# Two-layer graph attention on one core: a third buffer for the scaled features, the sums over A moved ahead at the end of the first pass, layer norm in two steps, and a row term in partial sums

## The chip, the cores and the metric

The kernel runs on one core of a Trainium2 chip. The metric is the device time of one execution in microseconds (us). The kernel before was timed three times: 2105.14, 2100.93 and 2103.20 us, median 2103.2 us.

## What is computed

Two layers over 4096 nodes with 512 features, each followed by a residual sum and a layer norm:

```python
feats = einsum('nf,hfo->hno', x, W)                 # 8 heads of 64
dense = s_self[:, :, None] + s_neigh[:, None, :]
dense = where(dense > 0, dense, 0.2 * dense) * A    # A: 4096 x 4096, zeros and ones
x = layernorm(x + relu(softmax(dense) @ feats + b)) # layer 0
q, k, v = x @ Wq.T + bq, x @ Wk.T + bk, x @ Wv.T + bv
a = where(mask, q @ k.T * scale, 0)                 # mask: same graph; 32 graphs of 128 nodes
scores = (a + A + A) * where(mask, 1, -1e6)
x = layernorm(x + (softmax(scores) * mask) @ v)     # layer 1
```

In layer 1 only the 32 diagonal blocks of 128 by 128 count. With M = Wq^T Wk the scores are x M x^T plus row terms; the one this change touches is `ub`, the product of bk with Wq, times the scale, needed as the same row of 512 numbers in all 128 partitions.

## The kernel before, in words

`adjacency_streamed_path` does the work; `general_path` is compiled but only entered for other kinds of input. Heads go in pairs: r = 0 to 3 is a pair, and a pass. In each pass the columns of A^T go in four chunks c of 1024, and in each chunk 32 tiles j of 128 rows.

**Setup** (lines 578 to 795). For each of eight blocks k of four tiles: load x, turn it (L635), multiply by W (L715, in `features`), add the bias into `fb` (L723). `scaled_features` (L726) makes two tiles from `fb`: `gst` (L729, VectorE) and `fst` (first half by ScalarE, L737, second half by VectorE, L738). Both are written to DRAM (`g_d`, `f_d`) by DMAs on GpSimd's queue (L750). `gst`, `fst`, `xT_f` and `pu_j` come from the pool `two` with two buffers; `fb` from `three` with three. The bits `exponentials` and `scores` for the attention need the copy `st` (L652) on ScalarE, and the small matmuls L658 read it. After blocks 3, 4 and 5 a load of four tiles of A, cast to fp8 (L573), goes into the same GpSimd queue.

**A pass** (`main_pass`, L1263). A step takes `wide` tiles j, eight in passes 0 to 2 and four in pass 3. In each step VectorE makes `q` (L1310) from `p_row`, `d_all` and the tile `at` of A^T; ScalarE (or VectorE, L1315) makes `mark` from `q`; TensorE accumulates `accf` (L1330) from `at` and `f_s`, then `acc` (L1347) from `q` and `g_s`, then `dens` (L1361) from the marks. In pass 0 it also accumulates `ae` (L1374) from `at`: the sums over A, written at the end of the step. `bring` gets the tiles `at` of the following step: in pass 0 by transposes (L1088) and copies (L1092), and for later passes by a load on SP's queue (L1078). In pass 0 half of these calls stand after `accf`, half at the end of the step, after `ae`. The twelve buffers of `at` (six in pass 3) go round; a buffer is free again when `accf`, `ae` and both `q` of its tile have been made.

**Ends of a chunk.** `sums_to_rows` first copies the accumulators (`ys` L1136 and L1144, `dcs` L1146, `aes` L1151), then hands back a generator of pieces, which are issued between the matmuls of the next chunk: `run_pieces` spends a credit of 0.75 us per tile and step, and each `yield` states a cost. During pass 1 the same credit pays for `weights_of_layer_1` (L864), whose last pieces are the column term `zb` (L908) and `ub` and `cb` (L918 to L929).

**Layer 1 in pass 3.** From the second chunk of pass 3 on, an order written out by hand is followed: `PLAN` names for each step what is issued after `accf` and what after `acc`. E ends a chunk and calls `rows_of_layer_0` (L1112: residual, relu, layer norm of four row tiles, made into `x1b`), R does so for its second half, a and b are the pieces of `layer_1` for these two. What is left after the last chunk is a string of the same letters (L1426). `rows_out` (L1039) writes rows, two tiles at a time, through `layernorm` (L518): statistics on VectorE (L524, L525), the power on GpSimd (L527, L528), the scaling on VectorE (L530).

**Order.** TensorE runs in the order of the source (L455). The other engines' orders, and those of the DMA queues, are fixed when the kernel is built, by a scheduler that works with modelled times and the order of the source.

```python
banks.append(banks.pop(0))          # misc(): PSUM banks in turn
queue = nc.sync if blk >= NT // 4 - 2 else nc.gpsimd   # rows_out: who writes the rows
for x_ in follow[first:]:           # end of a step: second half of the next tiles
    bring(*x_)
```

Of the kernel before, what the change touches and what calls it, by code (L numbers as in the profile page):

```python
# [10 lines left out]
F32 = mybir.dt.float32  # L11
BF16 = mybir.dt.bfloat16
# [7 lines left out]
P = 128  # L20
# [384 lines left out]
def adjacency_streamed_path(  # L405
# [112 lines left out]
    def layernorm(tiles):  # L518

        n = len(tiles)  # L520
        stats = small.tile([P, n, 6], F32, name="stats_f")
        mv = small.tile([P, n, 2], F32, name="mv_f")
        for u, src in enumerate(tiles):
            nc.vector.bn_stats(stats[:, u, :], src)  # L524
            nc.vector.bn_aggr(mv[:, u, :], stats[:, u, :])  # L525
        rstd = small.tile([P, n], F32, name="rstd_f")
        nc.gpsimd.tensor_scalar_add(rstd, mv[:, :, 1], EPS)  # L527
        nc.gpsimd.tensor_tensor(rstd, rstd, neg_half_4[:, :n], OP.pow)  # L528
        for u, src in enumerate(tiles):
            nc.vector.tensor_scalar(  # L530
                src, src, mv[:, u, 0:1], rstd[:, u : u + 1], op0=OP.subtract, op1=OP.mult
            )


    gfp = ctx.enter_context(tc.tile_pool(name="gs", bufs=2))
# [42 lines left out]
    with tc.tile_pool(name="setup1", bufs=1, side="right") as one, tc.tile_pool(  # L578
# [20 lines left out]
        for c in range(FC):  # L599
# [1 line left out]
                w_sb[:, c].rearrange("p (h o) -> p h o", h=H),  # L601
                W[:, ts(c, P), :].rearrange("h p o -> p h o"),
            )
        a_b2 = two.tile([P, PR, 2, FP], F32R, name="fst").bitcast(F32)
# [120 lines left out]

        def scaled_features(k, u, fb):  # L726
            j = 4 * k + u
            gst = two.tile([P, PR, 2, FH], F32, name="gst")
            nc.vector.tensor_tensor(  # L729
                gst.rearrange("p r h o -> p (r h) o"),  # L730
                fb,
                e_all[:, j, 1, :, None].to_broadcast([P, H, FH]),
                OP.mult,
            )
            fst = two.tile([P, PR, 2, FP], F32R, name="fst")
            fr = fb.rearrange("p (r h) o -> p r (h o)", h=2)
            nc.scalar.activation(fst[:, :, 0, :], fr, AF.Copy, scale=-1.0)  # L737
            nc.vector.scalar_tensor_tensor(  # L738
                fst[:, :, 1, :],
                fr,  # L740
                -1.0,
                fst[:, :, 0, :].bitcast(F32),
                op0=OP.mult,
                op1=OP.subtract,
            )
            for dst, n, src in (
                (g_d, FP, gst.rearrange("p r h o -> p r (h o)")),
                (f_d, 2 * FP, fst.rearrange("p r s n -> p r (s n)").bitcast(F32)),
            ):
                nc.gpsimd.dma_start(dst[:, k, :, ts(u, n)].rearrange("r p n -> p r n"), src)  # L750
# [113 lines left out]
    def weights_of_layer_1(keep, wp):  # L864

        L1["M"] = keep.tile([P, FC, F], F32, name="M_sb")
        L1["wvT"] = keep.tile([P, FC, F], F32, name="wvT")
        L1["zb"] = keep.tile([P, FC], F32, name="zb")
        L1["ub"] = keep.tile([P, F], F32, name="ub")
        L1["cb"] = keep.tile([P, 1], F32, name="cb")  # L870
        L1["bv"] = keep.tile([P, F], F32, name="bv_row")
        nc.sync.dma_start(L1["bv"], broadcast_rows(bv, P, F))
        cols = {}
        for name, v in (("q", bq), ("k", bk)):
            cols[name] = wp.tile([P, FC], F32, name="b_" + name)
            nc.sync.dma_start(
                cols[name],
                bass.AP(tensor=v.tensor, offset=v.offset, ap=[[1, P], [P, FC]]),
            )
        ws = {}  # L880
        for name, w in (("q", Wq), ("k", Wk), ("v", Wv)):
            yield 6.0
            ws[name] = wp.tile([P, FC, F], F32, name="w_" + name)
            nc.sync.dma_start(ws[name], w.rearrange("(c p) f -> p c f", p=P))
        yield 6.0
        for m in range(FC):
            pm = misc([P, F])
            for o in range(FC):
                nc.tensor.matmul(
                    pm,  # L890
                    ws["q"][:, o, ts(m, P)],
                    ws["k"][:, o, :],
                    start=(o == 0),
                    stop=(o == FC - 1),
                )
            nc.scalar.mul(L1["M"][:, m, :], pm, scale)
            yield 3.7
        for o in range(FC):
            pv = misc([P, FC, P])
            for k in range(FC):  # L900
                nc.tensor.transpose(pv[:, k, :], ws["v"][:, o, ts(k, P)], ident)
            nc.scalar.copy(L1["wvT"][:, :, ts(o, P)], pv)
            if o % 2:
                yield 1.3
        pz = misc([P, FC])
        for m in range(FC):
            for o in range(FC):
                nc.tensor.matmul(  # L908
                    pz[:, m : m + 1],
                    ws["k"][:, o, ts(m, P)],  # L910
                    cols["q"][:, o : o + 1],
                    start=(o == 0),
                    stop=(o == FC - 1),
                )
        nc.scalar.mul(L1["zb"], pz, scale)
        yield 2.0

        pu = misc([P, F])  # L918
        pc = misc([P, 1])
        kb = wp.tile([P, FC, P], F32, name="kb")  # L920
        nc.vector.tensor_copy(kb, cols["k"][:, :, None].to_broadcast([P, FC, P]))
        for dst, rhs in ((pu, ws["q"]), (pc, cols["q"][:, :, None])):
            for o in range(FC):
                nc.tensor.matmul(
                    dst, kb[:, o, :], rhs[:, o, :], start=(o == 0), stop=(o == FC - 1)
                )
        nc.scalar.mul(L1["ub"], pu, scale)
        nc.scalar.mul(L1["cb"], pc, scale)
        yield 4.5  # L929

    def layer_1(blk, x1b, lp, lp1, lp2):
# [107 lines left out]
        def rows_out(us):  # L1039
            ys = []  # L1040
            for u in us:
                po = misc([P, F])
                nc.tensor.matmul(po, pT[:, u, :], vs[u], start=True, stop=True)  # L1043
                y = lp.tile([P, F], F32, name="y_f")
                nc.vector.scalar_tensor_tensor(
                    y, po, rd[:, u : u + 1], x1b[:, u, :], op0=OP.mult, op1=OP.add
                )
                ys.append(y)
            layernorm(ys)
            for i, u in enumerate(us):  # L1050
# [14 lines left out]
        values(2)  # L1065
        values(3)
        yield
        rows_out((2, 3))
        yield


# [40 lines left out]
    def rows_of_layer_0(blk, hst, lp):  # L1112
        x1b = lp.tile([P, 4, F], F32, name="x1b")
        for u in range(4):
# [4 lines left out]
            for dst, src in (  # L1119
# [1 line left out]
                (x1b[:, u, F - FP :], hst[:, it % CT, :]),  # L1121
            ):
                nc.vector.scalar_tensor_tensor(dst, src, 0.0, dst, op0=OP.max, op1=OP.add)
        layernorm([x1b[:, u, :] for u in range(4)])
        return x1b

    def sums_to_rows(r, c, acc, accf, ae, u_row, later_by):
# [104 lines left out]

    PLAN = [("E", "b"), ("b", "b"), ("b", "a"), ("Ra", "a"), ("a", "b"), ("ba", "b")]
    PLANS = PLAN + [("ab", ""), ("aaba", "")], PLAN + [("a", ""), ("aa", "a")]
    plan = {"b": None}

    def run_plan(todo):
        for k in todo:  # L1240
            gen = ends[0] if k == "E" else plan[k]
            if gen is not None:
                next(gen)
            if k == "E":
                ends.pop(0)
# [17 lines left out]
    def main_pass(r, ae=None, wide=4):  # L1263

        for c in range(NCH):
# [10 lines left out]
            def pieces(c, group, place):  # L1276
                if r == PR - 1 and c:
                    run_plan(PLANS[c == NCH - 1][group][place])
                elif place == (r == 0):
                    run_pieces(0.75 * wide)  # L1280

            acc = psa.tile([P, 2, HB], F32, name="acc")
            accf = psa.tile([P, 2, HB], F32, name="accf")
            marks = {}
            for j0 in range(0, NT, wide):
# [41 lines left out]
                for j in cycle:  # L1327
                    for w in range(2):
                        for s in range(2):
# [4 lines left out]
                                start=(j == 0 and w == 0),  # L1334
                                stop=(j == NT - 1 and w == 1),
                            )
                first = wide // 2 if r == 0 or wide == 4 else 6
                for x_ in follow[:first]:
                    bring(*x_)
# [17 lines left out]
                for j in range(done_j - 8, done_j) if done_j % 8 == 0 else ():  # L1357
                    for s in range(2):
                        for h in range(2):
# [5 lines left out]
                                start=(j == 0),  # L1365
                                stop=(j == NT - 1),
                            )
                if r == 0:
                    for j in cycle:

                        a_j = ats[r, c, j].bitcast(BF16).rearrange("p (n k) -> p n k", k=2)
                        for s in range(2):
                            lo = 32 * (2 * (j % 2) + s)
                            nc.tensor.matmul(  # L1374
                                ae[lo : lo + NE + 1, :],
                                e_p[:, j, : NE + 1],
                                a_j[:, ts(s, HB), 1],
                                start=(j < 2),
                                stop=(j >= NT - 2),
                            )  # L1380
# [39 lines left out]
    with tc.tile_pool(name="lp", bufs=2) as lp, tc.tile_pool(  # L1420
# [2 lines left out]
        pools.update(lp=lp, lp1=lp1, lp2=lp2)  # L1423
        main_pass(3)
        plan["K"] = kind_of_inputs(lp1)
        run_plan("bbEbbbbaaRaaKKbbababaababbbb")  # L1426


@with_exitstack
# [50 lines left out]
```

## Time and profile before

| | |
|---|---|
| median of three executions | 2103.2 us (2100.93 to 2105.14) |
| the profiled execution, its own time | 2104.88 us |
| its span in the profile | 2102.9 us |
| TensorE (PE) busy | 2061.3 us, 98% of the span |
| VectorE (DVE) busy | 1659.0 us, 79% |
| ScalarE (ACT) busy | 1535.7 us, 73% |
| GpSimd (POOL) busy | 249.4 us, 12% |
| moved by DMA | 551 MB, mean 262 GB/s |
| setup | 0 to about 172 us |
| first `accf` of passes 0, 1, 3 | 177, 604, 1391 us |
| after the last chunk | 1981 to 2103 us |

In the profile a line names a source line, an engine, an operation, the tiles (out<-in), and then times. In the timeline the columns are start, busy time, engine, line, operation, tiles, count, and in brackets how long the engine had been idle before and what ended it. In a table of stretches there are, for each engine, busy us and (x) instructions, then PEclk, the share of full speed that TensorE's clock was granted, then the DMA's busy share and GB/s. SPq and POOLq are the queues in which SP and GpSimd issue DMAs. Float32 matmuls show as two instructions each.

### The profile page before, as it was taken

To read this page: it belongs to the slowest core of one execution; us is meant where nothing else is said; L and a number is where in the kernel's file an instruction comes from. 1 tells how busy PE (TensorE), PEld (TensorE's weight loads), DVE (VectorE), ACT (ScalarE), POOL (GpSimd) and SP (SyncE) were. 2 spreads that over 40 slices of the span, in tenths; PEclk is the share of its full clock that TensorE was granted. 3 is DMA by queue.
4 is the path that set the end of the run, shared out by engine and by line. 5 is a ranking of instruction groups with operands and counts; after the bars stand their busy time and mean duration, and the time that the engine had idled before them with its cause. 6 is when DMAs were issued, how large, how long until landed. Compare 5 with 4: busy or idle time off the path is not lost. (4 is left out here: it accounts for less than half of the span.)

```text
span 2102.9 us, 38131 instructions
## 1 busy us (share of the span) xinstructions
PE 2061.3 (98%) x15012; PEld 1015.0 (48%) x15012; DVE 1659.0 (79%) x2032; ACT 1535.7 (73%) x1818; POOL 249.4 (12%) x391
## 2 busy tenths in 40 slices
PE   8999999999999999999999999999999999999997
PEld 4545555454445544445444544444454444445443
DVE  5547788878788998787999989999975884886654
ACT  3327998888868889787899989998876666567420
POOL 2333222222100000000000000000300210210110
PEclk9999999999999999999999999999999999999999
DMA  8999999999889999887999999989964674675211
GB/s 246 270 211 243 287 285 271 294 263 278 263 286 327 338 361 344 297 301 239 323 324 343 311 327 337 334 281 362 305 238 152 239 243 144 225 270 163 73 48 42
DMA packets 207881, 551.28 MB, mean 262 GB/s; under 512 B 25292, under 2 KB 66252, under 8 KB 207692
## 3 DMA queue, kind: packets, MB, share of 16 engines
q1 hardware_dynamic: 140748, 425.79, 58.3%
q0 software_dynamic: 62784, 121.91, 23.3%
q8 instruction: 120, 1.97, 0.4%
q10 hardware_dynamic: 4160, 1.05, 0.2%
q14 instruction: 69, 0.57, 0.1%
HBM read 491.79 MB, written 107.22 MB: 285 GB/s over the span
## 5 line engine op out<-in xcount | busy, mean ns | idle before, releaser
L1310 DVE SCALAR_TENSOR_TENSOR q<-p_row,d_all,at 128x1024 f32<-128x1024 f32 x1024 | 1242.5, 1277 | 180.2 <-PE acc L1347 146.2
L1319 ACT ACTIVATE mark<-q,nb_all 128x1024 fp8e4<-128x1024 f32 x896 | 994.6, 1145 | 192.1 <-DVE q L1310 176.7
L1347 PE MATMUL acc<-q,g_s 128*32 128x512 f32 x8192 | 907.3, 594 | 3.3 <-DVE q L1310 2.9
L1347 PEld LDWEIGHTS acc<-q,g_s 128*32 128x32 f32 x8192 | 265.1, 110 | 599.2 <-issue 532.9
L1330 PE MATMUL accf<-at,f_s 128*128 128x512 f32 x2048 | 494.4, 397 | 5.5 <-DMA at<-at_d 3.9
L1330 PEld LDWEIGHTS accf<-at,f_s 128*128 128x128 f32 x2048 | 378.7, 188 | 116.0 <-issue 25.6
L1107 ACT ACTIVATE ck<-ck,neg_half_f 128x1024 f32<-128x1024 f32 x128 | 145.9, 1140 | 22.1 <-DMA ck<-in_adj_dram 22.1
L1108 ACT ACTIVATE ck<-ck,neg_quarter 128x1024 f32<-128x1024 f32 x128 | 146.3, 1143 | 1.8
L1092 ACT CAST at<-ps_m 128x1024 fp32r<-128x1024 fp8e4 x128 | 120.1, 1026 | 10.4 <-issue 5.9
L1361 PE MATMUL dens<-mark,e_b 128*6 128x512 fp8e4 x2048 | 125.0, 379 | 1.2 <-ACT mark L1319 1.2
L715 PE MATMUL ps_set<-w_sb_f,xT_f 128*128 128x512 f32 x256 | 116.4, 603 | 0.0
L957 PE MATMUL ps_m<-x1T,M_sb 128*128 128x512 f32 x256 | 113.1, 595 | 1.2 <-ACT x1T L938 1.2
L1029 PE MATMUL ps_m<-wvT,x1T 128*128 128x512 f32 x256 | 114.2, 594 | 0.0
L1212 POOL DMA_DIRECT2D hs_d<-hst x12 | 10.7, 895 | 849.6 <-DVE hst L1202 755.6
L1315 DVE TENSOR_SCALAR mark<-q,d_all 128x1024 fp8e4<-128x1024 f32 x128 | 95.7, 748 | 4.8
L737 ACT ACTIVATE fst<-fb 128x512 fp32r<-128x512 f32 x32 | 20.3, 633 | 101.5 <-DMA f_d<-fst 76.8
L1361 PEld LDWEIGHTS <-e_b 128*6 128x6 bf16 x2048 | 52.7, 86 | 81.0 <-issue 37.2
L1093 POOL DMA_DIRECT2D at_d<-at x128 | 68.7, 537 | 181.3 <-ACT at L1092 104.0
L957 PEld LDWEIGHTS ps_m<-x1T,M_sb 128*128 128x128 f32 x256 | 47.9, 190 | 62.7 <-issue 60.1
L1029 PEld LDWEIGHTS ps_m<-wvT,x1T 128*128 128x128 f32 x256 | 47.6, 190 | 57.2 <-issue 56.0
L715 PEld LDWEIGHTS ps_set<-w_sb_f,xT_f 128*128 128x128 f32 x256 | 49.1, 199 | 49.7 <-issue 49.4
L1037 DVE TENSOR_TENSOR v_t<-ps_m,bv_row 128x512 f32<-128x512 f32 x32 | 21.9, 684 | 62.2 <-PE ps_m L1029 62.2
(172 smaller groups left out, 1141.6 us busy)
## 6 DMA issues: line engine op xcount, KB each, us to landing
at<-at_d SPq DMA_DIRECT2D x384, 512.0 KB, 6.1
ck<-in_adj_dram SPq DMA_DIRECT2D x128, 512.0 KB, 5.4
f_s<-f_d SPq DMA_DIRECT2D x128, 512.0 KB, 7.6
at_d<-at POOLq DMA_DIRECT2D x128, 512.0 KB, 15.2
g_s<-g_d SPq DMA_DIRECT2D x128, 256.0 KB, 5.7
f_d<-fst POOLq DMA_DIRECT2D x32, 512.0 KB, 6.3
p_row<-pu_d SPq DMA_DIRECT2D x32, 512.0 KB, 7.1
a_b<-in_adj_dram POOLq DMA_DIRECT2D x32, 512.0 KB, 17.2
```

The source lines that it names most:

```text
L715: nc.tensor.matmul(pf, tile_j(xTs[k][:, c].rearrange("p u n -> p (u n)"), u), w_sb[:, c, :], start=(c == 0), stop=(c == FC - 1),)
L957: nc.tensor.matmul(pz, L1["M"][:, f, ts(c, P)], x1T[:, f, :], start=(f == 0), stop=(f == FC - 1),)
L1029: nc.tensor.matmul(pv, x1T[:, f, ts(u, P)], L1["wvT"][:, f, :], start=(f == 0), stop=(f == FC - 1),)
L1092: nc.scalar.copy(at, both[:, :, k])
L1107: tc.keep_in_program_order(nc.scalar.activation(ck, ck, AF.Square, bias=neg_half))
L1108: nc.scalar.activation(ck, ck, AF.Abs, bias=neg_quarter, accum_out=binp[:, k : k + 1])
L1310: nc.vector.scalar_tensor_tensor(q, p_row[h], d_j, ats[r, c, j].bitcast(F32), op0=OP.max, op1=OP.mult)
L1315: nc.vector.tensor_scalar(mark, q, d_j, None, op0=OP.is_gt, saturate=False)
L1319: nc.scalar.activation(mark, q, AF.Sigmoid, bias=nb_all[:, j, hh : hh + 1], scale=BIG, saturate=False,)
L1330: nc.tensor.matmul(accf[:, s, :], f_s[j // 4][:, j % 4, w, :], ats[r, c, j][:, ts(s, HB)], start=(j == 0 and w == 0), stop=(j == NT - 1 an ...
L1347: nc.tensor.matmul(acc[o : o + 32, s, :], g_s[j // 4][:, j % 4, h, o % FH : o % FH + 32], qs[j, h][:, ts(s, HB)], start=(j == 0), stop=(j ...
L1361: nc.tensor.matmul(dens[lo : lo + 6, :], e_b[:, j, 2 * r + h, :], marks[j, h][:, ts(s, HB)], start=(j == 0), stop=(j == NT - 1),)
```

## The change

Five edits:

1. `gst` and `fst`, and the tile at the start that shares `fst`'s buffers, come from `three` in place of `two`.
2. In the last step of the last chunk of pass 0 the matmuls into `ae` are issued straight after `accf`, ahead of `bring` and `acc`; in all other steps of pass 0 they stay where they were.
3. `layernorm` returns its last part, the four (or two) scalings L530, as a function. `rows_out` calls it at once. `rows_of_layer_0` stores it as `plan["F"]`, and the plan has a letter F: in the steps with E and R it comes after `acc`, after the last chunk straight behind E and R.
4. `ub` is made from four matmuls with 32 columns each, one for each chunk of Wq, into four strips of one bank (`pu`), a copy with the scale to SBUF (`part`), and one matmul with a matrix `pick` that adds rows 0, 32, 64 and 96; its `cb` matmuls go ahead of these. There is one more `yield 2.0`.
5. For the very last block `rows_out` is called twice with one tile in place of once with two.

```diff
-        for u, src in enumerate(tiles):
-            nc.vector.tensor_scalar(
-                src, src, mv[:, u, 0:1], rstd[:, u : u + 1], op0=OP.subtract, op1=OP.mult
-            )
+        def finish():
+            for u, src in enumerate(tiles):
+                nc.vector.tensor_scalar(
+                    src, src, mv[:, u, 0:1], rstd[:, u : u + 1], op0=OP.subtract, op1=OP.mult
+                )
+        return finish
...
-            gst = two.tile([P, PR, 2, FH], F32, name="gst")
+            gst = three.tile([P, PR, 2, FH], F32, name="gst")
...
-            fst = two.tile([P, PR, 2, FP], F32R, name="fst")
+            fst = three.tile([P, PR, 2, FP], F32R, name="fst")
...
-        for dst, rhs in ((pu, ws["q"]), (pc, cols["q"][:, :, None])):
-            for o in range(FC):
-                nc.tensor.matmul(
-                    dst, kb[:, o, :], rhs[:, o, :], start=(o == 0), stop=(o == FC - 1)
-                )
-        nc.scalar.mul(L1["ub"], pu, scale)
+        pu = misc([P, F])
+        for o in range(FC):
+            nc.tensor.matmul(
+                pc, kb[:, o, :], cols["q"][:, o : o + 1], start=(o == 0), stop=(o == FC - 1)
+            )
+        for o in range(FC):
+            nc.tensor.matmul(
+                pu[32 * o : 32 * o + 32, :], kb[:, o, :32], ws["q"][:, o, :], start=True, stop=True
+            )
+        part = ws["v"][:, 0, :]
+        nc.scalar.mul(part, pu, scale)
+        pick = ws["v"][:, 1, :P]
+        nc.vector.memset(pick, 0.0)
+        for o in range(FC):
+            nc.vector.memset(pick[32 * o : 32 * o + 1, :], 1.0)
+        yield 2.0
+        pu = misc([P, F])
+        nc.tensor.matmul(pu, pick, part, start=True, stop=True)
+        nc.scalar.copy(L1["ub"], pu)
         nc.scalar.mul(L1["cb"], pc, scale)
         yield 4.5
...
-            layernorm(ys)
+            layernorm(ys)()
...
-        rows_out((2, 3))
+        if blk == NT // 4 - 1:
+            rows_out((2,))
+            rows_out((3,))
+        else:
+            rows_out((2, 3))
...
-        layernorm([x1b[:, u, :] for u in range(4)])
+        plan["F"] = layernorm([x1b[:, u, :] for u in range(4)])
...
-    PLAN = [("E", "b"), ("b", "b"), ("b", "a"), ("Ra", "a"), ("a", "b"), ("ba", "b")]
+    PLAN = [("E", "Fb"), ("b", "b"), ("b", "a"), ("Ra", "Fa"), ("a", "b"), ("ba", "b")]
...
+                if r == 0 and (c, j0 + wide) == (NCH - 1, NT):
+                    sums_over_a(c, cycle)
                 first = wide // 2 if r == 0 or wide == 4 else 6
                 for x_ in follow[:first]:
                     bring(*x_)
...
-                if r == 0:
-                    for j in cycle:
...
+                if r == 0 and (c, j0 + wide) != (NCH - 1, NT):
+                    sums_over_a(c, cycle)
                 for x_ in follow[first:]:
                     bring(*x_)
...
-        run_plan("bbEbbbbaaRaaKKbbababaababbbb")
+        run_plan("bbEFbbbbaaRFaaKKbbababaababbbb")
```

`sums_over_a` holds the lines of the loop over `ae` that stood at the end of the step, unchanged.

More of the change, by code (lines that the diff above doesn't have):

```diff
@@ L603, in adjacency_streamed_path @@
             )
-        a_b2 = two.tile([P, PR, 2, FP], F32R, name="fst").bitcast(F32)
+        a_b2 = three.tile([P, PR, 2, FP], F32R, name="fst").bitcast(F32)
         a_b2 = a_b2.rearrange("p r s n -> p (r s n)").rearrange(
@@ L916, in weights_of_layer_1 @@
         yield 2.0
-        pu = misc([P, F])
         pc = misc([P, 1])
@@ L1240, in run_plan @@
         for k in todo:
+            if k == "F":
+                plan[k]()
+                continue
             gen = ends[0] if k == "E" else plan[k]
@@ L1280, in pieces, with sums_over_a @@
                     run_pieces(0.75 * wide)
+            def sums_over_a(c, cycle):
+                for j in cycle:
+                    a_j = ats[r, c, j].bitcast(BF16).rearrange("p (n k) -> p n k", k=2)
+                    for s in range(2):
+                        lo = 32 * (2 * (j % 2) + s)
+                        nc.tensor.matmul(
+                            ae[lo : lo + NE + 1, :],
+                            e_p[:, j, : NE + 1],
+                            a_j[:, ts(s, HB), 1],
+                            start=(j < 2),
+                            stop=(j >= NT - 2),
+                        )
             acc = psa.tile([P, 2, HB], F32, name="acc")
@@ L1367, in main_pass @@
                             )
-                if r == 0:
-                    for j in cycle:
[L1371 to L1380, printed above, removed]
+                if r == 0 and (c, j0 + wide) != (NCH - 1, NT):
+                    sums_over_a(c, cycle)
                 for x_ in follow[first:]:
```

## The prediction

> **What bounds the kernel now.** I read the page first, then the list of waits of TensorE, then tables of short stretches, and the timeline wherever TensorE had a gap.
>
> ```profile
> PE 2061.3 (98%) x15012; PEld 1015.0 (48%) x15012; DVE 1659.0 (79%) x2032; ACT 1535.7 (73%) x1818; POOL 249.4 (12%) x391
> PE   8999999999999999999999999999999999999997
> ```
>
> TensorE is the bound nearly everywhere: 2061.3 of 2102.9 us. Only its gaps can be won: 41.6 us, of which the start before the first features (about 8) and the end after the last matmul (13) belong to no queue. What is left sits in a few places, and the edits point at four of them. Setup, chain of one stall (timeline), and the clock after it (stretches of 5 us):
>
> ```profile
> 113.59 0.63 ACT L737 ACTIVATE fst<-fb 128x512 fp32r<-128x512 f32 x1 [9.82 <-DMA f_d<-fst]
> 114.13 0.57 ACT L652 COPY st<-ps_set 128x512 f32<-128x512 f32 x1
> 114.75 1.89 PE L658 MATMUL ps_set<-stack,st 128*128 128x16 f32 x8 [3.70 <-ACT st L652]
> ...
> 115.00:120.00 5.00, 5.00 (x25) 5.00 (x26) 4.95 (x15) 3.45 (x13) 4.55 (x6) 0.50 0.68 202
> ```
>
> ScalarE sits 9.82 us in front of an `fst` buffer whose write hasn't landed; `st` is queued behind it, and TensorE needs `st`. The stall costs twice: 3.70 us of nothing, then half clock. In stretches of 1 us the clock is 0.88, 0.50 (six times), 0.71 from 114 to 122.
>
> End of pass 0 and start of pass 1:
>
> ```profile
> 604.25 0.45 SPq L1272 DMA_DIRECT2D u_row<-pu_d  x1
> 604.32 3.90 PE L1330 MATMUL accf<-at,f_s 128*128 128x512 f32 x16 [0.73 <-PE ae L1374]
> 604.87 3.04 SPq L1078 DMA_DIRECT2D at<-at_d  x4
> ...
> 611.09 3.77 PE L1330 MATMUL accf<-at,f_s 128*128 128x512 f32 x12 [2.87 <-DMA at<-at_d]
> ...
> 615.88 1.19 PE L1330 MATMUL accf<-at,f_s 128*128 128x512 f32 x4 [1.01 <-DMA at<-at_d]
> ```
>
> Four tiles `at` are loaded only once `ae` (to 603.6) and the `u_row` load are out of the way; TensorE waits for them twice. First E of pass 3, and the piece with `ub`:
>
> ```profile
> 1506.03 1.91 DVE L530 TENSOR_SCALAR x1b<-x1b,mv_f,rstd_f 128x512 f32<-128x512 f32 x4 [1.25 <-POOL rstd_f L528]
> 1507.86 8.46 DVE L1310 SCALAR_TENSOR_TENSOR q<-p_row,d_all,at 128x1024 f32<-128x1024 f32 x7
> ...
> 1509.19 7.81 PE L1347 MATMUL acc<-q,g_s 128*32 128x512 f32 x46 [2.45 <-DVE q L1310]
> ...
> 965.13 4.12 PE L908 MATMUL ps_m<-b_q,w_k 128*128 128x1 f32 x32
> 969.12 6.55 PE L924 MATMUL ps_m<-w_q,kb 128*128 128x512 f32 x8
> 975.51 0.95 PE L924 MATMUL ps_m<-b_q,kb 128*128 128x1 f32 x8
> ```
>
> VectorE waits 1.25 us for GpSimd, scales for 1.91 us, and only then makes the `q` that `acc` wants. And L924 runs at half speed: the clock is 0.50 from 968.5 to 974.5, after 4 us of one-column matmuls.
>
> **What the Trainium skill says.** "TensorE: Matmul & The Clock Gate", Part 1: the clock has two states, 1.2 and 2.4 GHz, switched by windows of about 3.4 us of low or high activity. The trace agrees on the half clock (0.50) but shows 6.0 to 6.5 us of it in three places, and a fall during one-column matmuls, not only in idleness. "TensorEngine Tiling (Array Packing)", Theoretical Speedup: up to 4x with 32 columns. It agrees: 64 of L1347 in 7.00 us are 0.109 us each, 16 of L957 in 6.87 us are 0.43. "Trainium Kernel Development and Optimization", Key Constraints: the DMAs of all queues share the same 16 engines. It fits: `f_d` writes take 4.0 us at best and 15.6 at worst, the worst while a load of A is under way (DMA share 1.18 at 105 to 110).
>
> **Part by part** (minus is a gain)
>
> *Third buffer.* From where a tile of `gst` or `fst` is reused after two tiles it is now after three; work is unchanged. In the stall, `fst` of tile (k,2) waited for the write of (k,0), issued at 97.9. With three it waits for (k-1,3)'s, which landed at 103.1, before its features are done (104.4). `st` follows at about 105. The next, (k,3), still waits until 113.5, but what TensorE needs of ScalarE then is later: it has features (k+1,0) to 111.05, L658, L635 and features (k+1,1) to go on with, about 6.6 us, and seven PSUM banks hold them. So 3.70 goes, and with it the half clock: L658 1.89 for 1.05, L635 3.65 for 1.95, L715 4.43 for 3.60, together 3.4. With 0.24 at 155.5 this makes 7.3. What is late next is the DMA: between 95 and 165 its share averages 0.93; the same work in 7 us less needs 1.03, and in the blocks with loads of A about 1.2, above the 1.18 seen. I take 5.0 of the 7.3; bounds -7.3 and 0, and as no instruction is added, +1 for a less lucky place of a load. GpSimd's queue issues the writes earlier in the same order; no wait is added. The start's tile that shares `fst`'s buffers is read by VectorE only until 19.4: 0.
>
> *Sums over A first.* The 16 matmuls (1.08 us) move from behind `dens` to ahead of `acc`: no work, and in that step `acc` starts 1.08 us later. The end stays at 603.6, and the next `accf` is held by `ys` L1136 (ends 604.2), so nothing is won or lost there. But the four `at` buffers are now free when their `q` are made: the eight first `q` of this step are done at 589.1, `ae` would be at 587.0. So SP can issue the loads some 15 us earlier, if the build puts them ahead of `u_row`. Then `accf` of 32 matmuls takes 7.6 us, as at 578.4, and ends at 612.0 for 617.0. Behind it `acc` has seven `q` ready; VectorE's small reductions (612 to 615, 2.9 us) no longer lie in an idle stretch and may cost 0.6. So -5.0 + 0.6 = -4.4; bounds -5.0 and 0.
>
> *Layer norm in two steps.* Same 4 x 0.48 us, later. The 2.45 at 1506.7 goes as far as `q` goes ahead of L530: wait 1.25 and scaling 1.91 exceed it, but VectorE is full there (47.1 of 50 us), so the 1.91 comes back into the same stretch. -1.9; bounds -2.45 (all) and +1.9 (one scaling ends up in front of another `q`). At the other five places TensorE has no gap from this: E and R of the next chunks show 0.2 us of waits, for `hst`. In the tail F follows at once: 0. `x1b` is first read two steps later, about 40 us, so that cover is wide.
>
> *Row term.* Removed: 8 x 0.43 = 3.44 us of full clock, 6.4 as run. Added: 8 x 0.109 = 0.87, a copy to SBUF on ScalarE of 0.60 (as L927) plus about 0.2 for the two hand-overs, in which TensorE stands still, and 2 x 0.43 = 0.86; memsets on VectorE, idle there for 13.5 us, 0. By the stated costs the pieces fit into the same step (credit 5.4, then 3.4, 1.4), so the copy is not hidden. At half clock: `cb` 1.9, strips 1.75, gap 0.8, sum 1.72 = 6.2 for 7.2 before: -1.0, if the clock comes back at the same moment. If strips, gap and one-column work keep it low one window longer, half of 3.4 us is lost: +0.7. I take -0.2, with -1.0 and +1.7 as bounds.
>
> *Last block.* One tile's chain for two: after the last matmul (2089.5) the second copy of L1045, L524, L525, L527, L528 and L530 remains, but the first scaling no longer stands in front of the second (0.48), and the first row's DMA is issued early. The one-tile power is new: between 0 and the 0.72 of two. -0.5; bounds -1.0 and +0.3.
>
> Sum: -5.0 - 4.4 - 1.9 - 0.2 - 0.5 = -12.0. The profiled execution took 2104.9 (2.0 more than its span), so it would take 2092.9; the median of the runs is 1.7 below it, 2103.2, so I forecast 2091.2. Behind each stall work on TensorE is dense, with DVE at 47 of 50 us in passes 1 and 2, so what is won isn't given back.
>
> **Rivals.**
> - *A: as summed*, 2091.2; from 2086 (all ends at their best, -17) to 2095. 55%.
> - *B: the setup is held by the DMA.* The writes compete with the loads of A and the stall only moves. Speaks for it: share 1.18 in the stall. Against: 0.04 to 0.5 of share right after it. -7.0: 2096.2. 15%.
> - *C: the loads stay behind `u_row`.* The edit then doesn't do what it could: `u_row` waits for L1136 until 604.2 and blocks SP's queue. For it: that is the order before. Against: the first four were issued at 577.4, as soon as free. -7.6: 2095.6. 14%.
> - *B and C together*, -2.6: 2100.6, within 0.2%. 9%.
> - *D: slower.* TensorE's clock does not come back under 32-column work. Every return of the trace's half clock was under 128-column matmuls; after the new piece `acc` follows. Then `acc` runs 13.9 us longer, `dens` 1.8, and half a window of `accf` 1.7: +17.4 on -12.0, 2108.6; it decides from 12 us of such clock. Against: `acc` never lost the clock in 14 us. 7%.
>
> About 0.2%, 4.2 us, is what a measurement of this kernel can tell from no change. A, B and C are faster: with some doubt for orders newly chosen by the build, 0.85; same 0.08; slower 0.07. Range: A to B and C, and part of the joint case: 2086 to 2099.5; left out are D, most of the joint case, and little below.
>
> **What would show it.** Third buffer: no wait of ScalarE L737 for `f_d` near 9 us, clock 1.00 from 110 to 125, first `accf` near 172. Sums: L1078 issued before 600, L1330 at 604 unbroken. Layer norm: no 2.45 at 1507. Row term: strips near 1.8 us and a gap of 0.8 before the sum; watch the clock in the following `acc`. Wrong would be: a setup as long as before, SP's `at` loads still after `u_row`, or stalls at new places of pass 3.

## The result, and the profile after

| | before | after |
|---|---|---|
| median of the runs | 2103.8 us (6 runs, 2100.93 to 2105.14) | 2090.45 us (6 runs, 2087.96 to 2094.48) |
| the profiled execution, its own time | 2104.88 us | 2089.37 us |
| its span | 2102.9 us | 2087.0 us |

The ratio is 0.994, with a 95% interval of 0.9927 to 0.9953: 13.4 us less, where 12.0 had been forecast. Where the two profiles differ shows best at events that both have (start of the event, us; the last column is what the stretch since the event above gained):

| event | before | after | gained |
|---|---|---|---|
| first `accf` of pass 0 | 177.01 | 168.91 | 8.1 |
| last `accf` of pass 0 | 578.39 | 569.54 | 0.8 |
| first `acc` of pass 1 | 617.00 | 603.98 | 4.2 |
| the column term's one-column matmuls (before L908) | 965.13 | 951.31 | 0.8 |
| the `dens` behind the row term | 990.14 | 975.20 | 1.1 |
| first `accf` after the first E of pass 3 | 1500.17 | 1485.63 | -0.4 |
| the last four matmuls (before L1043) | 2088.49 | 2073.20 | 0.8 |
| end of the span | 2102.9 | 2087.0 | 0.6 |

Two stretches carry the gain. The page of after: of the 15.9 us, 6.0 are busy time of TensorE (2061.3 before) and the rest gaps.

```profile
PE 2055.3 (98%) x15014; PEld 1011.8 (48%) x15014; DVE 1659.8 (80%) x2037; ACT 1537.4 (74%) x1819; POOL 251.0 (12%) x393
```

Setup of after, timeline at the place of the stall (columns: start, duration, engine, line, operation, and in brackets the idle time before it and what ended it). Lines have moved: `st` is L656, the matmuls behind it L662, the first half of `fst` L741.

```profile
102.90 0.63 ACT L741 ACTIVATE fst<-fb 128x512 fp32r<-128x512 f32 x1 [3.35 <-DVE fb L727]
103.44 0.57 ACT L656 COPY st<-ps_set 128x512 f32<-128x512 f32 x1
...
110.33 1.00 PE L662 MATMUL ps_set<-stack,st 128*128 128x16 f32 x8
...
112.28 0.63 ACT L741 ACTIVATE fst<-fb 128x512 fp32r<-128x512 f32 x1 [7.76 <-DMA f_d<-fst]
```

ScalarE still waits 7.76 us for a write of `f_d`, but one tile later: `st` is done at 104.0, six us before TensorE wants it. In the stretches (columns: stretch, length, busy time and count of PE, PEld, DVE, ACT, POOL, clock, DMA share, GB/s) the clock is whole. The DMA share from 100 to 150 is 1.04, for 0.96 before:

```profile
105.00:110.00 5.00, 5.00 (x13) 2.26 (x12) 0.69 (x1) 0.00 (x0) 0.85 (x2) 1.00 1.13 267
...
115.00:120.00 5.00, 5.00 (x16) 2.20 (x14) 4.37 (x14) 1.81 (x5) 3.10 (x5) 1.00 1.05 297
```

End of pass 0 and start of pass 1; the first line is the last `accf` of pass 0 before, the others are the timeline of after:

```profile
578.39 7.57 PE L1330 MATMUL accf<-at,f_s 128*128 128x512 f32 x32
...
568.58 11.80 SPq L1099 DMA_DIRECT2D at<-at_d  x8
569.54 7.58 PE L1368 MATMUL accf<-at,f_s 128*128 128x512 f32 x32
...
577.05 1.09 PE L1312 MATMUL ae<-at,e_p 128*25 128x512 bf16 x16
577.96 13.91 PE L1388 MATMUL acc<-q,g_s 128*32 128x512 f32 x128
578.21 0.09 DVE L847 MEMSET new<- 1x32 f32 x1 [3.41 <-PE ae L1312]
...
596.41 1.59 SPq L1296 DMA_DIRECT2D u_row<-pu_d  x2
596.48 7.56 PE L1368 MATMUL accf<-at,f_s 128*128 128x512 f32 x32 [1.76 <-issue]
...
603.98 2.35 PE L1388 MATMUL acc<-q,g_s 128*32 128x512 f32 x20
```

(The last row ends where the window of the timeline ends, not with `acc`.) The loads of `at` (L1099) now stand ahead of `u_row`, and the 32 `accf` run in one piece, 7.56 us. `ae` stands ahead of the last `acc` of pass 0 and makes it 0.9 us later; so the table counts this stretch from the `accf` ahead of both. VectorE's small reductions begin at 578.2, in a hole of 3.41 us that waits for `ae`.

The first E of pass 3, timeline of after:

```profile
1491.49 1.91 DVE L532 TENSOR_SCALAR x1b<-x1b,mv_f,rstd_f 128x512 f32<-128x512 f32 x4 [1.26 <-POOL rstd_f L528]
1493.32 8.45 DVE L1348 SCALAR_TENSOR_TENSOR q<-p_row,d_all,at 128x1024 f32<-128x1024 f32 x7
1494.66 7.46 PE L1388 MATMUL acc<-q,g_s 128*32 128x512 f32 x46 [2.46 <-DVE q L1348]
```

That is the picture of before: a wait for GpSimd of 1.26 (1.25), the four scalings in 1.91, TensorE idle for 2.46 (2.45), and behind that 3.4 us of half clock (from 1494.8; before from 1510.8).

The column and row terms, timeline of after:

```profile
951.31 3.63 PE L912 MATMUL ps_m<-b_q,w_k 128*128 128x1 f32 x32
954.80 1.20 PE L928 MATMUL ps_m<-b_q,kb 128*128 128x1 f32 x8
...
955.93 1.93 PE L932 MATMUL ps_m<-w_q,kb 128*32 128x512 f32 x8
...
958.58 2.08 PE L943 MATMUL ps_m<-w_v 128*128 128x512 f32 x2 [0.72 <-ACT w_v L936]
960.58 14.79 PE L1388 MATMUL acc<-q,g_s 128*32 128x512 f32 x128
```

Strips 1.93, gap 0.72, sum 2.08, nearly all at half clock (955.5 to 962.3), and the `acc` behind takes 14.79 for 13.94: the half clock reaches into it.

### The profile page after: what moved, and what is told of

It reads as the page before. It is cut to its first block, busy times and chain, and to the rows that moved or that the text cites. A ratio compares the mean times of both kernels' runs of the same rounds, so it can differ in the third digit from the quotient of the medians.

```text
span 2087.0 us, 38127 instructions
## 1 busy us (share of the span) xinstructions
PE 2055.3 (98%) x15014; PEld 1011.8 (48%) x15014; DVE 1659.8 (80%) x2037; ACT 1537.4 (74%) x1819; POOL 251.0 (12%) x393
## 5 line engine op out<-in xcount | busy, mean ns | idle before, releaser
L741 ACT ACTIVATE fst<-fb 128x512 fp32r<-128x512 f32 x32 | 20.4, 637 | 86.1 <-DVE fb L727 52.1
## 6 DMA issues: line engine op xcount, KB each, us to landing
at_d<-at POOLq DMA_DIRECT2D x128, 512.0 KB, 14.7
```

## Experiments

Each ran beside runs of the kernel before. "Alone" means the kernel before with one edit.

### The third buffer alone

```diff
-            gst = two.tile([P, PR, 2, FH], F32, name="gst")
+            gst = three.tile([P, PR, 2, FH], F32, name="gst")
...
-            fst = two.tile([P, PR, 2, FP], F32R, name="fst")
+            fst = three.tile([P, PR, 2, FP], F32R, name="fst")
```

> The kernel before with only the third buffer (gst, fst, and the tile at the start). Theory: the setup's whole shortening comes from this edit, and no DMA limit takes any of it back: first accf 8.1 us earlier (about 169 in place of 177.0), and the total shorter by the same 8, ratio about 0.996. Rival (the prediction's discount): the DMA takes some back, 5.0 us, ratio 0.9976, and the rest of what the changed kernel gains here comes from another edit.

Measured: 2096.18 us (5 runs, 2095.81 to 2098.37), ratio 0.9958, interval 0.9944 to 0.9971. The first `accf` starts at 168.96, as in after. At the pass boundary the old wait for `at` is still there, 3.53 us (before 2.87 and 1.01; timeline of this kernel):

```profile
594.57 0.45 SPq L1272 DMA_DIRECT2D u_row<-pu_d  x1
...
599.39 9.27 SPq L1078 DMA_DIRECT2D at<-at_d  x8
602.09 6.79 PE L1330 MATMUL accf<-at,f_s 128*128 128x512 f32 x16 [3.53 <-DMA at<-at_d]
```

So all of the setup's gain is this edit's, and none of the boundary's.

### The sums over A first, alone

```diff
+                if r == 0 and (c, j0 + wide) == (NCH - 1, NT):
+                    sums_over_a(c, cycle)
```

> The kernel before with only the sums over A moved ahead in the last step of pass 0. Theory: from that step's acc to the first acc of pass 1 the time falls by 5.1 us (31.1 to 26.0), because the four loads of at are issued right when ae is done and no accf waits for them; ratio about 0.9976. Rival (the prediction): 0.6 us of that is lost to VectorE's small reductions, 4.4 us. Second rival: the loads stay behind u_row without the other edits, 0.

Measured: 2098.93 us (8 runs, 2094.57 to 2102.18), ratio 0.9968, interval 0.9954 to 0.9982. Setup keeps its stall (first `accf` at 178.40); from the last `accf` of pass 0 to the first `acc` of pass 1 it takes 34.46 us, as in after (34.44) and 4.2 less than before (38.61). Counted from the last `acc` it would look like 5.1 (26.04 for 31.11), but 0.9 of that is `ae`, which has only moved out of that stretch. The six profiles without the edit take 38.6 to 40.1 us, mean 39.4, so the pair of the table shows less than the average of 5.0. Timeline of this kernel:

```profile
605.73 7.59 PE L1344 MATMUL accf<-at,f_s 128*128 128x512 f32 x32 [1.76 <-issue]
```

### The row term alone

```diff
+        for o in range(FC):
+            nc.tensor.matmul(
+                pu[32 * o : 32 * o + 32, :], kb[:, o, :32], ws["q"][:, o, :], start=True, stop=True
+            )
...
+        nc.tensor.matmul(pu, pick, part, start=True, stop=True)
```

> The kernel before with only the row term made in partial sums. Theory from the trace of the changed kernel: from the end of the column term's matmuls to dens of the same step 1.1 us less; the half clock lasts as long as before (about 7 us) and reaches 2 us into acc; total 1 us shorter, ratio 0.9995, not to be told from none in time. Rival: half clock a window longer, total 1 to 2 us longer.

Measured: 2106.58 us (13 runs, 2103.05 to 2108.89), ratio 1.0002, interval 0.9993 to 1.001: no difference that this measurement can tell. In its profile the stretch from the column term to `dens` is 23.94 us, 1.07 less than before (25.01), as in after (23.89):

```profile
969.59 3.63 PE L908 MATMUL ps_m<-b_q,w_k 128*128 128x1 f32 x32
973.08 1.03 PE L924 MATMUL ps_m<-b_q,kb 128*128 128x1 f32 x8
...
974.04 1.71 PE L928 MATMUL ps_m<-w_q,kb 128*32 128x512 f32 x8
...
976.45 2.08 PE L939 MATMUL ps_m<-w_v 128*128 128x512 f32 x2 [0.70 <-ACT w_v L932]
978.46 15.25 PE L1360 MATMUL acc<-q,g_s 128*32 128x512 f32 x128
```

The piece from L924 to `acc` is 5.38 us for 7.27; `acc` gives back 1.31 (15.25 for 13.94), since the half clock, 974.3 to 981.2, ends only inside it. The 25.0 us of before hold for five of the six profiles with the old row term; in the sixth, the one with a third buffer for `fst` alone, the clock did not fall and the same stretch took 21.6. So the new order gains 1.1 us where the clock falls in both, and the old one without the fall is faster than it.

### Layer norm's scalings one step later

The edit as it stands, alone on the kernel before, builds a program with the same instructions in the same order on all five engines; it only moves lines of the source, and the scheduler puts the scalings back where they were. To see what the edit was to do, the version after was given a fixed order for these scalings, one step later:

```diff
-                nc.vector.tensor_scalar(
+                ins = nc.vector.tensor_scalar(
...
+                if n == 4:
+                    tc.keep_in_program_order(ins)
...
-    PLAN = [("E", "Fb"), ("b", "b"), ("b", "a"), ("Ra", "Fa"), ("a", "b"), ("ba", "b")]
+    PLAN = [("E", "b"), ("b", "Fb"), ("b", "a"), ("Ra", "Fa"), ("a", "b"), ("ba", "b")]
```

> The changed kernel, with the first letter F one step later in the plan (after acc of the step behind E) and the scaling held to its place in the source. In the changed kernel the built order of VectorE is the same as before at all scalings of the first layer norm, so the letter does nothing. Theory: once the scaling really stands behind the q, the wait of acc for q at the first E (2.46 us) goes, and the total falls by about 2.5 us against the changed kernel: 2088, ratio to before 0.9926. Rival: VectorE is full there, the 1.91 us land ahead of another q, and the wait only moves: 0.

Measured: 2086.5 us (4 runs, 2084.44 to 2088.54), ratio to before 0.991, interval 0.9893 to 0.9927. Timeline of this kernel at the first E:

```profile
1490.12 9.62 DVE L1350 SCALAR_TENSOR_TENSOR q<-p_row,d_all,at 128x1024 f32<-128x1024 f32 x8
1490.62 9.46 PE L1390 MATMUL acc<-q,g_s 128*32 128x512 f32 x62
...
1500.32 1.91 DVE L532 TENSOR_SCALAR x1b<-x1b,mv_f,rstd_f 128x512 f32<-128x512 f32 x4
1502.17 3.92 PE L1370 MATMUL accf<-at,f_s 128*128 128x512 f32 x16
```

The scalings start without a wait, behind all `q` of the step, `acc` has no gap that the timeline marks, and there is no half clock here. From the `accf` ahead of this `acc` (1486.77) to the one behind it (1502.17) it is 15.40 us, for 18.57 in after and 18.91 before: 3.2 us, more than the 1.9 that had been forecast. VectorE sets the pace of this `acc` (eight `q` in 9.62 us, 62 matmuls in 9.46, where 64 took 7.00 elsewhere), and it was spared both what stood ahead of its `q`: 1.26 us of waiting for GpSimd and 1.91 of scaling, 3.17 together.

### The third buffer for one of the two tiles

```diff
             gst = two.tile([P, PR, 2, FH], F32, name="gst")
...
-            fst = two.tile([P, PR, 2, FP], F32R, name="fst")
+            fst = three.tile([P, PR, 2, FP], F32R, name="fst")
```

> The kernel before with a third buffer for `fst` alone; `gst` keeps two. Theory: ScalarE's wait in front of `fst` was the whole cause of the stall, so the first `accf` of pass 0 starts at 169 (before 177.0, both buffers 169.0), and no stall of several us in front of L658 (here L655). Rival: the write of `gst` is nearly as late, VectorE then waits for it, and a good part of the stall comes back: first `accf` at 172 or later.

### No load of A in the later blocks of setup

```diff
-            if k in (3, 4, 5):
+            if k in ():
                 tc.keep_in_program_order(load_adjacency(0, 4 * (k - 3)))
```

> The kernel before, two buffers, but the three loads of A that it issues during setup are left out of setup and come when pass 0 asks for them; all else is computed. Theory of the prediction: a load of A that is under way is what makes the `f_d` write take 10 to 15 us, so with no load in setup the writes stay below 9 us and ScalarE's 9.8 us in front of `fst` falls below 4, with less than 1 us of stall in front of L658; the start of pass 0 then waits for A, so the time is not faster. Rival: two buffers are too few by themselves: the stall of 3 us or more in front of L658 and the half clock behind it stay.

Measured, one execution each: 2102.21 us with `fst` alone, 2120.89 without the early loads, beside 2108.84 for a run of before. The times of single runs tell little; the blocks of setup tell more. Between the matmuls L658 of successive blocks lie 18.47 us if nothing is in the way (us; the last two rows are the two kernels of single executions):

| kernel | blocks 3 to 4 | 4 to 5 | 5 to 6 | 6 to 7 | first `accf` |
|---|---|---|---|---|---|
| before | 19.38 | 22.33 | 21.83 | 18.92 | 177.01 |
| sums alone (two buffers) | 20.46 | 21.77 | 22.05 | 19.21 | 178.40 |
| after | 18.47 | 18.46 | 18.47 | 18.47 | 168.91 |
| third buffer alone | 18.92 | 18.47 | 18.47 | 18.47 | 168.96 |
| third for `fst` only | 22.08 | 18.47 | 19.10 | 19.92 | 174.95 |
| no load of A in later blocks | 22.41 | 18.47 | 18.46 | 18.47 | 190.61 |

With `fst` alone the large stall (4 to 5, and the half clock after it) is gone, so ScalarE's wait was its cause; but 169 was missed. VectorE now waits for the write of `gst`, in 11 places, 35.8 us in all, and holds ScalarE and later TensorE with it (timeline of this kernel):

```profile
106.73 0.63 ACT L737 ACTIVATE fst<-fb 128x512 fp32r<-128x512 f32 x1 [3.58 <-DMA f_d<-fst]
...
115.15 0.69 DVE L729 TENSOR_TENSOR gst<-fb,e_all 128x512 f32<-128x512 f32 x1 [8.73 <-DMA g_d<-gst]
...
117.13 0.63 ACT L737 ACTIVATE fst<-fb 128x512 fp32r<-128x512 f32 x1 [8.80 <-DVE fb L723]
```

That costs 0.6 and 1.5 us in the last two columns: the rival was right in kind, for a part. The other edit did not do quite what was meant: the build put the three loads of A at the very start, not into pass 0. W, loaded beside them, came late, and setup with it by 16 us. But from 35 us on no load of A is under way, and the stall is gone though both tiles have two buffers. Where before had waits of 9.82, 9.56 and 7.40 us for `f_d`, the longest left is the second line here (timeline of that kernel); the 4 us forecast as its upper end was too low, and one of 8.99 at 87.9, where before had 8.08 with no load of A under way either, costs nothing. The writes of `f_d` did not all stay below 9 us either: three, before 117, took 9.9 to 11.1, those after it at most 8.2:

```profile
1.39 1.15 POOL L573 DMA_DIRECT2D a_b<-in_adj_dram  x1 [0.33 <-issue]
...
121.35 0.63 ACT L737 ACTIVATE fst<-fb 128x512 fp32r<-128x512 f32 x1 [4.80 <-DMA f_d<-fst]
```

So, by one profile of each of the two kernels, the stall needs both: writes slowed by a load of A, and only two buffers. The first column is something else. There TensorE waits for a load of x (L594), in code that no edit touches. With two buffers for both tiles it lost 0.9, 2.0, 3.6 and 5.9 us in four kernels, with three for both 0 to 0.8 in six. It comes with `fst` alone and without loads of A too; why a third buffer for both takes it away was not settled.

### The last block alone

```diff
-        rows_out((2, 3))
+        if blk == NT // 4 - 1:
+            rows_out((2,))
+            rows_out((3,))
+        else:
+            rows_out((2, 3))
```

> The kernel before with the last block's two rows sent out one by one and nothing else. Theory: from the last L1043 to the last scaling 6.5 us (before 6.27), from there to the end of the span 7.3 (before 8.14), together -0.6. Rival: the second row's own chain and second DMA cost as much as they save, together within 0.2 of before's 14.41.

Measured, one execution: 2110.84 us beside 2108.84. From the last matmuls to the last scaling 6.5 us (before 6.3), from there to the end 7.8, together 14.3: the rival is right. Over all profiles of this study the sum is 13.2 to 14.7, mean 13.9, in the six without this edit, and 13.8 to 14.3, mean 14.0, in the six with it. The 0.6 in the table at the top is a spread of the last transfer, not a gain. The chain is 0.2 us longer each time, and the profile of after shows where:

```profile
2077.50 0.55 DVE L532 TENSOR_SCALAR y_f<-y_f,mv_f,rstd_f 128x512 f32<-128x512 f32 x1 [0.37 <-POOL rstd_f L528]
2077.96 0.17 DVE L525 BATCH_NORM_AGGREGATE mv_f<-stats_f 128x2 f32<-128x6 f32 x1
...
2078.53 0.58 POOL L528 TENSOR_TENSOR rstd_f<-rstd_f,neg_half 128x1 f32<-128x1 f32 x1
2079.14 0.55 DVE L532 TENSOR_SCALAR y_f<-y_f,mv_f,rstd_f 128x512 f32<-128x512 f32 x1 [1.01 <-POOL rstd_f L528]
```

The second row's L525 stands behind the first row's scaling, which itself waited for GpSimd; and the one-row power takes 0.58 for the 0.71 of two.

### The one-column matmuls spread out

```diff
         for m in range(FC):
+            pz = misc([P, 1])
+            for o in range(FC):
+                nc.tensor.matmul(
+                    pz,
...
+            nc.scalar.mul(L1["zb"][:, m : m + 1], pz, scale)
             pm = misc([P, F])
```

> The version with the scaling one step later, with the 32 one-column matmuls of `zb` spread in four groups of eight ahead of the four pieces of `M`, `cb` at the end of the piece before, and the strips, copy and sum in steps of their own. Theory: 3.6 us of one-column matmuls in a row are what halves the clock, so here it stays at 1.00 from the weights' pieces through the next `acc`: strips 0.9 instead of 1.93, sum 1.0 instead of 2.08, `acc` of that step 14.0 instead of 15.0; with `cb` 3 us less than the version with the scaling alone (2083.5). Rival: the clock falls because of the strips or of the gap before the sum, whatever precedes them: then strips or sum still run at half clock and less than 1.5 us is won.

### The same at the end of setup

```diff
             scaled_features(k, 0, fbs[0])
+            if k == NB - 1:
+                sums_of_features(0)
```

(and so on for the other three tiles; `sums_of_features` makes one of four columns)

> The same, and the 32 one-column matmuls of the sum of features at the end of setup in four groups of eight between the last four tiles' features. Theory: here too the run of 3.6 us is the cause, so no half clock between the end of setup and the first 32 `accf` of pass 0 (before and after: some 6 to 8 us of it): about 3.5 us less than with the first spreading alone (2080). Rival: the clock falls there for the gaps in front of the first transposes of A, which stay; then the half clock stays and nothing is won.

### The spread results taken by VectorE

```diff
-            nc.scalar.mul(L1["zb"][:, m : m + 1], pz, scale)
+            nc.vector.tensor_scalar(L1["zb"][:, m : m + 1], pz, scale, None, op0=OP.mult)
```

> The version with the 32 one-column matmuls of `zb` spread over the pieces of `M`, but VectorE instead of ScalarE takes the four results out of PSUM; no spreading in setup. Theory: what the spreading gave back was the first of these copies, which stood behind three `mark` on ScalarE (TensorE waited 1.7 us in front of `M`'s first matmuls, and some 3 us of half clock came after it); VectorE is idle there, so the wait falls below 0.5, the clock stays at 1.00, and the stretch from the `accf` at 787 to the one at 1001 of the version with the scaling alone (214.4 us there, 214.2 with ScalarE's copies) falls to 211. Span near 2078. Rival: VectorE's own queue of `q` holds the copies as long, and the stretch stays at 214.

Measured: 2083.27 us (4 runs, 2082.9 to 2083.47, ratio to before 0.9897, interval 0.9881 to 0.9914) for the first, 2084.63 (4 runs, 2083.24 to 2086.42, 0.9901, 0.9885 to 0.9918) with the setup too, 2082.07 (4 runs, 2080.89 to 2083.68, 0.9901, 0.9883 to 0.992) with VectorE. All three beat both kernels of this case; among themselves, and against the 2086.5 of the later scaling, the ratios don't part them.

Around the weights the profiles do. In the first, the clock stays at 1.00 from `cb` through `acc`, but the stretch between two `accf` that frames the weights' pieces is 214.2 us for 214.4 without the spreading. What was won is given back at the first group (timeline of the first):

```profile
816.03 3.21 ACT L1356 ACTIVATE mark<-q,nb_all 128x1024 fp8e4<-128x1024 f32 x3
...
816.73 0.95 PE L897 MATMUL ps_m<-b_q,w_k 128*128 128x1 f32 x8
819.15 0.15 ACT L904 ACTIVATE zb<-ps_m 128x1 f32<-128x1 f32 x1
819.35 5.40 PE L907 MATMUL ps_m<-w_k,w_q 128*128 128x512 f32 x8 [1.67 <-ACT zb L904]
```

The copy of `zb` stands behind three `mark` on ScalarE, TensorE stands for 1.67 us, and 3.4 us of half clock follow (L907 takes 5.40 for 3.68). With VectorE, timeline of the third:

```profile
820.34 3.70 PE L907 MATMUL ps_m<-w_k,w_q 128*128 128x512 f32 x8 [0.25 <-DVE zb L904]
...
957.63 1.06 PE L932 MATMUL ps_m<-w_q,kb 128*32 128x512 f32 x8
...
981.50 1.02 PE L943 MATMUL ps_m<-w_v 128*128 128x512 f32 x2
```

Strips 1.06, sum 1.02, no gap, and the stretch is 211.0 us, as forecast; the span is 2079.6. So the spreading keeps the clock whole. But 3.6 us of one-column matmuls in a row do not always halve it. The kernel with a third buffer for `fst` alone has them in a row too, and its clock stays at 1.00 (timeline and stretch of that kernel):

```profile
965.53 3.63 PE L908 MATMUL ps_m<-b_q,w_k 128*128 128x1 f32 x32
969.01 3.68 PE L924 MATMUL ps_m<-w_q,kb 128*128 128x512 f32 x8
...
962.00:990.00 28.00, 28.00 (x229) 14.68 (x228) 17.74 (x17) 19.64 (x24) 0.00 (x0) 1.00 0.69 240
```

The last section says what parts the two cases.

At the end of setup the same edit did nothing: there the rival was right. TensorE also stands 2.08 and 0.81 us in front of the first transposes of A, for ScalarE's casts, and that suffices (stretches of the second kernel):

```profile
164.00:169.00 5.00, 2.10 (x22) 1.82 (x20) 4.67 (x7) 5.00 (x6) 3.59 (x6) 0.65 0.71 239
169.00:174.00 5.00, 5.00 (x18) 4.01 (x17) 5.00 (x5) 4.97 (x6) 1.40 (x4) 0.67 1.02 374
```

## Why the prediction was right, and which of its steps were not

The forecast, 2091.2, lies 0.7 from the measured 2090.45, and the likeliest case, all parts as summed, is the one that came. That it lies so near is luck: in the pair of profiles setup and the row term gave 4.0 us more than was taken, layer norm and the last block 2.4 less.

- **Third buffer: mechanism right, size too small.** Taken was -5.0; measured -8.1 in this pair, and -9.9 between the means of four profiles with two buffers (178.7) and six with three (168.8), of which 2.9 are the wait for x. The working had found 7.3 and then struck 2.3 off with "What is late next is the DMA". That step failed. The share did rise as worked out there (1.03 from 95 to 158; at most 1.14 in five us with a load under way, where 1.2 had been worked out), and ScalarE did wait for `f_d` again, 7.76 us; but with three buffers the wait falls behind `st`, where nothing TensorE needs is queued. What the pair shows above 7.3 is about the 0.9 us of the wait for x, which had not been counted at all.
- **Sums over A first: right in mechanism and size, two small terms wrong.** -4.4 was taken; measured -4.2 in this pair and alone, -5.0 between the means of six profiles each. The loads gave 5.2 (the `accf` take 7.50 us to the next `acc`, for 12.68), for the 5.0 put down. "Nothing is won or lost there" was wrong: the next `accf` follows the last `acc` of pass 0 by 18.4 us before and 18.5 after, and `ae` makes that `acc` 0.9 later, so 1.0 is lost. The +0.6 for VectorE's small reductions did not come: they moved up into the hole before `q` (578.2), since what they wait for, `ae`, was ready 16.6 us earlier, counted from that step's `accf`.
- **Layer norm in two steps: failed.** -1.9 was taken and nothing came. The step assumed that the built order follows the line's new place; it doesn't, the program of this edit alone is the old one. That the edit doesn't do what it says had been a rival only for the loads, not here. The later scaling shows that the place itself was worth 3.2 us, outside the bound of 2.45: the working took the 1.91 of scaling, but the wait for GpSimd goes too, and the half clock behind the gap was not in it.
- **Row term: mechanism right, size a little small.** -0.2 was taken, between -1.0 and +1.7; measured -1.1 alone and together, just outside, and only against profiles of the old order in which the clock fell. In after `cb` took 1.20 for the 1.9 put down, the strips 1.93 for 1.75, the gap 0.72 for 0.8, the sum 2.08 for 1.72; the clock came back late, as feared, but that cost only 0.9 to 1.3 us of `acc`. Not in the working: the clock fell later, 4.2 us after the first one-column matmul for 3.0 before, so L912 and most of L928 ran at full speed (L908 had taken 4.12, L912 takes 3.63). That too depends on where a grid of 3.41 us falls (last section). The half clock of before lasts from 968.1 to 974.9, not from 968.5 to 974.5, and all three long ones take 6.8 us, not 6.0 to 6.5.
- **Last block: wrong in size.** -0.5 was taken; it is 0. The chain became 0.2 us longer, and the second, smaller transfer ends no earlier on the average.
- **Rivals.** The DMA did not hold the setup (B), the loads did not stay behind `u_row` (C). In D the clock does come back under 32-column work: after the row term it is 0.50 until 962.3 and 1.00 from then on, with `acc` the only work. The trace of before had already shown it, against the sentence that every return was under 128-column matmuls: from 1510.8 to 1514.2 the clock is 0.50, TensorE does nothing but `acc`, and behind it the clock is 1.00.
- **The rest.** "Only its gaps can be won" does not hold: 6.0 of the gain is busy time, and the working itself counts such time behind the stall and in the row term. In the pair of profiles the span falls by 15.9 us; 13.4 are the setup, the boundary and the row term; 0.6 is the end's spread. What is left, +0.8, +0.8, -0.4 and +0.8 in long stretches, was not put down to an edit; the first of them, pass 0 up to its last `accf`, takes 399.8 to 403.5 us over the twelve profiles, and no edit touches it. The profile of before lay 1.1 above the median of its six runs, that of after 1.1 below.

## What to carry to other kernels

A stall is made by what is queued behind the waiting instruction: one more buffer for both tiles of a producer took TensorE's stall away though the DMA stayed as busy and ScalarE still waits, while one for only one of them moved the wait to the next engine. If a scheduler fixes the engines' orders, compare the built order before costing a moved line, for a move in the source may be none. A stretch must be counted from an event that the edit does not shift. And if single profiles differ by half a microsecond at the end of a transfer, look at more of them before it goes on an account.

## What the runs showed of the hardware that was not expected

The clock can fall though TensorE is 100% busy, if what it does is one-column matmuls. Whether it falls depends on where they lie on a grid of fixed steps that runs through the whole execution. In before the half clock starts at 114.76, 172.78, 968.09 and 1510.81; these lie 17, 233 and 159 times 3.413 us apart, and it lasts 6.83, 6.83, 6.83 and 3.41 us, two steps or one. In the other eleven profiles, too, all starts within one execution lie whole steps apart, but the grid lies differently in each.

Nine profiles have the 32 one-column matmuls in a row. In eight of them one-column work filled 2.2 to 3.4 us of one step (2.96 before, where the step is 964.68 to 968.09 and they begin at 965.13; 3.41 after; the least, 2.20, with the sums alone), and the clock fell at the end of that step. In the ninth (`fst` alone) they begin at 965.53, where the steps are 964.05 to 967.46 and on to 970.87; they filled 1.93 and 1.69 us of the two, and the clock stayed. So in these nine profiles the limit lies between 1.9 and 2.2 us of a step of 3.41. Idle time adds to it: a group of 0.95 us with the gap of 1.67 behind it halved the clock (819.6), with a gap of 0.25 it did not.

The Trainium skill ("TensorE: Matmul & The Clock Gate", Part 1) speaks of idle and busy windows of about 3.4 us; these runs fit the length, if one-column matmuls count as idle, and show that less than a whole window of them suffices. A DMA share of 1.13 over 5 us held nothing up that was needed.
